# Four cross-attention layers in one kernel: layer 1 on a thread of its own, layer 2's weights folded, and new durations in the kernel's planner

## The chip, the cores and the metric

The kernel runs on one core of one Trainium2 chip. The metric is the device time of one execution, in microseconds (us). The core has a matrix engine (TensorE, "PE" in the profile; its weight loads are shown as "PEld"), a vector engine (VectorE, "DVE"), a scalar engine (ScalarE, "ACT"), a general engine (GpSimd, "POOL") and a queue that issues the transfers (SyncE, "SP"). Matrix products end in PSUM, a memory of eight banks; everything else lies in SBUF.

## The reference

`x` has 64 batches of 128 tokens by 128 features; the context `ctx` has 64 batches of 77 tokens by 128. Four layers follow each other, all in f32. Cut to what is computed:

```
# layer 0, 16 heads of 8
Q = x @ Wq.T + bq;  K = ctx @ Wk.T + bk;  V = ctx @ Wv.T + bv
s = where(causal, Q_h @ K_h.T / sqrt(8), -1e9)
x = layer_norm(softmax(s) @ V_h + x);  x = gelu(x @ W1.T + b1) @ W2.T + b2 + x
# layer 1, 16 heads of 8
s = where(mask, -inf, (q_h @ k_h.T / sqrt(8)) * attention_weights)   # both 64 x 16 x 128 x 77
x = layer_norm(x + (softmax(s) @ v_h) @ Wo.T + bo)
# layer 2, 16 heads of 8, one 8 x 8 matrix wq, wk, wv shared by all heads
s = where(mask == 0, -1e20, (x_h @ wq) @ (ctx_h @ wk).T)
a = layer_norm((softmax(s / sqrt(128)) @ (ctx_h @ wv)) @ w_out + b_out + x)
x = layer_norm(relu(a @ w_ff1 + b1) @ w_ff2 + b2 + a)
# layer 3, 16 heads of 64 over x itself, in segments of 64 tokens
q, k, v = split(rms_norm(x) @ to_qkv);  q, k = rope(q), rope(k)
x = x + softmax(mask(q @ [mem, persist, k].T / 8)) @ [mem, persist, v] @ to_out
x = x + (silu(g) * a) @ ff_w2 + b2,  a, g = split(rms_norm(x) @ ff_w1 + b1)
```

## The kernel before

The 64 batches are worked on in 16 groups of four. Within a group a layer's projections and its feed-forward run on all four batches at once (512 columns), its attention batch by batch.

**The planner.** The program is not written in the order in which it runs. Layers are Python generators. Each engine call is recorded by `Plan`, which gives it a time: `Plan.matmul` for PE (line 150), `Plan.other` for the other engines (line 237), from durations written down in those functions. `issue` (line 295) then emits every engine's instructions by planned time, and each engine runs its own list in that order. A generator yields what it needs next: `"wait"` and a condition, `"also"` and a new generator (a new thread), or a tile shape of PE with the tiles that must be ready. The loop at the end (line 1378) takes the thread whose need is met first. There are two chains of threads: chain 0 is layers 0 to 2, chain 1 is layer 3. The variable `ahead` (line 1380) weighs them, so that chain 0 stays `LEADS` groups of work in front, with `WORK` as one group's work. Where the planner expects PE to stand for over `FILL` = 0.4 us, `keep_busy` (line 198) puts in filler products that nothing reads (`mm<-first,ident` in the profile, 512 or 128 columns), in the tile shape of the product that is waited for.

**Tile shapes of PE.** A product with 32 rows of weights uses a quarter of the array (shape 32x128); 64x64, 128x64 and 128x32 occur too. `Plan.switch` (line 217) charges a change of shape.

**Layers 0 to 2.** `layers_0_to_2` (line 1296) is one thread: for each group it runs `layer1(g)`, then `layer0_attention(g + 1)` (for groups past the first three; groups 1 and 2 have a thread and tiles of their own, `early_layer0`), then `layer2(g)`. Outputs and feed-forwards are threads that it starts. All three use one set of tiles, `own` (line 443), and `attend` (line 663) lets the values of one attention begin only when those of the attention before it are through (`tiles.ready`).

**Attention.** `attend` makes, per batch, a masked copy of the keys (`keys_of`, POOL line 673), then twice (eight heads each) `scores`: two products of 32 rows each into two PSUM banks (line 705, f32, which PE runs in two passes), from one of two pairs of banks (tag `sc`). The penalty of masked keys is added by products first (line 696): in layer 2 with 32 rows of weights, in layer 0 with the full 128 rows (the identity times the causal penalty, both bf16), so the shape changes between the two lines. Then DVE takes the maximum (line 717) and subtracts it (line 718), and ACT takes the exponential of 616 columns (line 721). Layer 1 has `first` (line 1021) ahead of that, for each half: multiply by the weights (line 1022), overwrite masked places (line 1024). `values` turns the scores on PE (line 656), copies them with ACT (line 657), multiplies with the values (line 740), copies (line 749), turns back (line 755), and DVE normalises (lines 760 and 762).

**Layer 2's weights.** wq, wk and wv are laid out as block diagonals; keys, values and queries are projected (lines 612, 623, 642), and `w_out` is applied in `layer2_output`.

**Layer 3's values** (line 1131): the first 64 tokens are copied by ACT straight into `vext`, the other 64 into `vs` (line 1132) and from there into `vext` by a transfer (line 1133). Two transfers bring the memory's row (line 1136).

The planner's durations for DVE and ACT in the kernel before; `hidden` is the part of an instruction that the next on the same engine may overlap, also where it needs the first one's result:

```
        elif engine == "DVE":
            cost, hidden = 0.15 + n * (0.0066 if op == "reciprocal" else 0.00104), 0.075
...
        elif engine == "ACT":
            cost, hidden = 0.157 + n * 0.00083, 0.06
...
            own, end = t + takes, t + cost
```

Of the kernel before, what the change touches and what calls it, by code (L numbers as in the profile page):

```python
# [12 lines left out]
F32 = mybir.dt.float32  # L13
# [7 lines left out]
P = 128  # L21
# [32 lines left out]
WORK = 71.0  # L54
LEADS = (1.60, 1.60, 1.20, 1.60, 1.60, 1.60, 1.60, 1.60, 1.60, 1.30, 1.40, 1.60, 1.60, 1.60, 1.60, 1.60)


class Plan:
# [8 lines left out]
    SWITCH = {  # L67
        (128, 128): {(128, 64): 0.093, (64, 64): 0.092, None: 0.094},
        (32, 128): {None: 0.267},
        (128, 64): {(128, 128): 0.13, None: 0.15},  # L70
        (64, 64): {None: 0.13},
        (128, 32): {None: 0.174},
    }

    def __init__(self):
        self.records = []
        self.lines = {}
        self.past = {}
        self.free = {}
        self.tags = {}  # L80
        self.pe, self.shape, self.work = 0.7, (128, 128), 0.0
        self.window, self.use, self.clock = 0.0, 0.0, 1.0
        self.known = {}
        self.idle = None
        self.lost, self.switched, self.fills = 0.0, 0.0, 0
        self.block = 0.0, 0.0
# [63 lines left out]
    def matmul(self, dst, w, x, passes, call, line):  # L150
# [7 lines left out]
        if shape[0] == 32:  # L158
            cost *= 0.3125
        elif shape[0] == 64:  # L160
            cost = max(cost / 4, 0.028)
        elif shape[1] == 32:
            cost /= 4
        elif shape[1] == 64:
            cost = max(cost / 2, 0.028)
        else:
            cost = max(cost * 1.02, 0.05 if half else 0.109)
        cost *= passes
        self.work += cost
# [7 lines left out]
        self.run(start, shape, cost, call, line, self.waits("PE", ends))  # L177
        end = self.pe + (0.2 if self.clock == 1.0 else 0.3)
# [4 lines left out]
    def run(self, start, shape, cost, call, line, extra=0.0):  # L183
# [11 lines left out]
        self.pe = start + switch + cost  # L195
        self.shape = shape

    def keep_busy(self, until, shape, line):

# [17 lines left out]
    def switch(self, shape):  # L217
        if shape == self.shape:
            return 0.0
        costs = self.SWITCH[self.shape]  # L220
        return costs.get(shape, costs[None])
# [15 lines left out]
    def other(self, engine, op, args, kw, call, line):  # L237
# [7 lines left out]
        elif engine == "DVE":  # L245
            cost, hidden = 0.15 + n * (0.0066 if op == "reciprocal" else 0.00104), 0.075
            cost += {"stream_shuffle": 0.05, "scalar_tensor_tensor": 0.06}.get(op, 0.0)
            cost += 0.105 if op == "copy_predicated" else 0.0
        elif engine == "ACT":
            cost, hidden = 0.157 + n * 0.00083, 0.06  # L250
# [3 lines left out]
        else:  # L254
            cost, hidden = 0.05 + n * 0.0024, 0.02
            if op == "tensor_tensor" and n <= G:
                cost = 1.02
# [31 lines left out]
        else:  # L289
            own, end = t + takes, t + cost  # L290
# [54 lines left out]
def four_layers(ctx: ExitStack, tc: tile.TileContext, a: dict, out: bass.AP):  # L345
# [10 lines left out]
    def pool_of(name, dtypes={}, space=None, **tiles):  # L356
# [5 lines left out]
    store = pool_of("store", xs=(4, G * P))  # L362
# [5 lines left out]
        "att", {"fm": U8, "mi": I32}, kb=(2, CT), s=(3, H * S2), fm=(2, H * S2),  # L368
        s3=(2, H * KE), sT=(1, 12 * P), sT3=(1, H * P), w=(2, 2 * P), mi=(1, CT),
    )  # L370
    act = pool_of(
        "act", {"part": BF16}, xT=(2, G * P), x3=(2, G * P), o=(2, G * P), y=(1, G * P),
        y3=(2, G * P), part=(1, P),
# [69 lines left out]
    own = Tiles(  # L443
        xT=(act, "xT"), kT=(proj, "kT"), v=(proj, "v"), qT=(proj, "qT"), o=(act, "o"),
        kb=(att, "kb"), s=(att, "s"), sT=(att, "sT"), w=(att, "w"),
    )

# [161 lines left out]
    def keys_values(cT, wk, bk, wv, bv, name, tiles=own):  # L609
        yield F, cT, "mm"  # L610
        pk = bank([P, CT], f"{name}_pk")
        matmul(pk, wk, cT, start=True, stop=True)
        kT = tiles.tile("kT", [P, G, S2], f"{name}_k")
        if bk is None:
            acte.copy(kT.rearrange("p b k -> p (b k)"), pk)
        else:
# [5 lines left out]
        for b in range(G):  # L622
            matmul(pv[:, b, :], cT[:, b * S2 : (b + 1) * S2], wv, start=True, stop=True)
        v = tiles.tile("v", [S2, 4, G, QR], f"{name}_v")
        pv = pv.rearrange("p b (f w) -> p f b w", f=4)
        if bv is None:
            acte.copy(v, pv)
        else:
            bv = bv.rearrange("p (f w) -> p f w", f=4).unsqueeze(2)
# [33 lines left out]
    def attend(qT, kT, va, pen, load, first, scale, name, tiles=own):  # L663
# [7 lines left out]
        def keys_of(b):  # L671
            kbs[b] = tiles.tile("kb", [P, QD, S2], f"{name}_{b}_kb")
# [7 lines left out]
        def scores(b):  # L680
            n = f"{name}_{b}"
            kb, s = kbs[b], ss[b]
            if b + 1 < G:
                keys_of(b + 1)
            mx = small.tile([P, H], F32, tag="mx", name=f"{n}_mx")
            for half in range(2):
                h0 = 8 * half
                yield F if pen is not None and pen(b)[2] == P else (32, 128), kb, qT, s, "sc"
                pb = two_banks(f"{n}_ps{half}")
                ps = pb[:, :, : QD * S2].rearrange("p c (i k) -> p c i k", k=S2)  # L690
                if pen is not None:
                    for c in range(2):
                        r = slice(QR * (2 * half + c), QR * (2 * half + c) + pen(b)[2])
                        if pen(b)[2] == P:
                            r = slice(0, P)
                        matmul(
                            ps[:, c],
                            pen(b)[0][r],
                            pen(b)[1][r].unsqueeze(1).to_broadcast([r.stop - r.start, QD, S2]),
                            start=True,  # L700
                            stop=False,
                        )
# [11 lines left out]
                if first is not None:  # L714
                    first(b, h0, d, ps)
                    ps = d
                dve.tensor_reduce(m, ps, AX.X, ALU.max)  # L717
# [66 lines left out]
        keys_of(0)  # L784
# [17 lines left out]
    pen0 = load("c_causal0", [P, S2])  # L802
# [6 lines left out]
    pen016 = const.tile([P, S2], BF16, tag="pen016", name="pen016")  # L809
    dve.tensor_copy(pen016, pen0)  # L810

    def pen_causal(b):
        return ident16, pen016, P
# [37 lines left out]
    fed = [0]  # L851

    def layer0_feed_forward(g, o, ready):
# [8 lines left out]
        fed[0] = g + 1  # L862


    begun0 = layer0_attention(0, *inputs0)
# [17 lines left out]
    def block_diagonal(name):  # L883
        rep = load(name, [P, DH])
        t = const.tile([P, H, DH], F32, tag=f"d_{name}", name=f"d_{name}")
        pool.tensor_tensor(
            t,
            rep.unsqueeze(1).to_broadcast([P, H, DH]),
            hmask.unsqueeze(2).to_broadcast([P, H, DH]),
            ALU.mult,  # L890
        )
        return t.rearrange("p h d -> p (h d)")

    wq2, wk2, wv = (block_diagonal(f"L2_{x}") for x in ("wq", "wk", "wv"))
    wv2 = const.tile([P, 4, 4, DH], F32, tag="wv2", name="wv2")
    for f, (h, step) in enumerate(FOURS):
        pool.tensor_copy(
            wv2[:, f], wv.rearrange("p (h d) -> p h d", d=DH)[:, h : h + 3 * step + 1 : step]
        )
    wv2 = wv2.rearrange("p f g d -> p (f g d)")  # L900
    wo2 = load("L2_w_out", [P, 1, P], a["L2_w_out"].unsqueeze(1))
# [13 lines left out]
    pen3 = load("c_causal3", [P, KE])  # L915
    pen316 = const.tile([P, KE], BF16, tag="pen316", name="pen316")
    dve.tensor_copy(pen316, pen3)
    wmem = load("L3_to_mem_tokens_w", [P, P])
# [15 lines left out]
    def memory_tokens():  # L934
# [16 lines left out]
        vmem = const.tile([B, H, DH3 + 1], F32, tag="vmem", name="vmem")  # L951
# [4 lines left out]
        mn = const.tile([B, P], F32, tag="mn", name="mem_n")  # L956
        acte.activation(mn, pm, AF.Copy, scale=1.0 / S2)
        sq = const.tile([B, P], F32, tag="sq", name="mem_sq")
# [8 lines left out]
        pooled = const.tile([P, B], F32, tag="mn2", name="mem_pooled")  # L967
# [4 lines left out]
        tokT = const.tile([P, B], F32, tag="mn3", name="mem_tokT")  # L972
# [7 lines left out]
        dve.memset(vmem[:, :, DH3], float(NM))  # L980
        for c in range(2):
            yield F, tokT, "mm"
# [499 lines left out]
```

## Time and profile before

| | us |
|---|---|
| median of 3 runs (2543.57 to 2558.1) | 2552.77 |
| span of the profiled execution, first to last instruction | 2548.2 |
| PE busy in it | 2406.2 |
| DVE busy | 1893.3 |
| ACT busy | 1412.2 |
| POOL busy | 1286.6 |

The profile gives for each group of instructions its source line, engine, operation, the tiles written and read, its shape and count, then the summed busy time and the mean duration of one in ns, then the idle time of the engine ahead of them and what ended it. PE's products are pipelined, so their durations overlap: what one costs is read from the distance between starts, not from its duration. Only idle time of the engine that sets the end costs anything.

PE's instruction list of the program before has 16,470 products, of which 489 are fillers (372 of 512 columns, 117 of 128), and 1155 changes of tile shape. SP issues 745 transfers.

### The profile page before, as it was taken

What the parts mean: (1) busy time and instruction counts of PE and PEld (TensorE: products, weight loads), DVE (VectorE), ACT (ScalarE), POOL (GpSimd) and SP (SyncE); (2) the same over time, 40 slices, a digit from 0 to 9 for tenths busy, and PEclk for the clock granted to TensorE, in tenths of its full rate; (3) what the DMA queues carried; (4) which work ended last, traced back from release to release, by engine and by line L of the source; (5) the groups of instructions that cost most, each with busy time, mean ns of one, the idle gap of its engine ahead of it and who ended that gap; (6) DMA issues with size and microseconds to landing.
All of it is one profiled execution on the core that took longest, in us unless ns stands there. A gap on an engine that the chain in (4) does not pass through costs nothing.

```text
span 2548.2 us, 64630 instructions
## 1 busy us (share of the span) xinstructions
PE 2406.2 (94%) x26657; PEld 1786.3 (70%) x26657; DVE 1893.3 (74%) x3952; ACT 1412.2 (55%) x2489; POOL 1286.6 (50%) x1290
## 2 busy tenths in 40 slices
PE   7999999999999999999999999999999999999998
PEld 4565776768677677677676776777767667767776
DVE  3756886967868678786877768687787868867765
ACT  3454556565565645556565655656556565554553
POOL 2234554645555546453564546455455554536653
PEclk9999999999999999999999999999999999999999
DMA  5412212111121121212112121211112112120000
GB/s 111 122 33 44 65 20 46 46 34 39 43 43 42 35 48 25 67 21 56 35 27 62 25 65 21 51 39 40 41 32 51 34 35 55 21 60 13 14 22 15
DMA packets 376768, 108.23 MB, mean 42 GB/s; under 512 B 329027, under 2 KB 365208, under 8 KB 376344
## 3 DMA queue, kind: packets, MB, share of 16 engines
q1 hardware_dynamic: 376472, 104.08, 18.2%
q8 instruction: 210, 3.44, 0.6%
q14 instruction: 86, 0.70, 0.1%
HBM read 74.97 MB, written 4.19 MB: 31 GB/s over the span
## 4 chain that ended last, share of the span: by engine, by line
PE 53%; DVE 28%; issue 6%; POOL 5%; ACT 4%; DMA 2%; SPq 1%; DVEq 0%; POOLq 0%; ACTq 0%
PE mm L656 8%; PE sc L705 5%; PE mm L1099 5%; DVE mx L717 5%; PE mm L590 4%; PE sc L1195 3%; PE sc L845 3%; DVE s L718 3%; PE mm L740 3%; DVE s L1024 3%; PE mm L1226 2%; DVE s L1022 2%; DVE ro L1101 2%; PE mm L1129 2%; DVE mx L1167 2%
## 5 line engine op out<-in xcount | busy, mean ns | idle before, releaser
L657 ACT COPY sT<-mm 116x512 f32<-116x512 f32 (+2 forms) x832 | 442.8, 585 | 147.5 <-PE mm L656 138.6
L1102 POOL TENSOR_TENSOR ro<-ro,w_c_sin 128x512 f32<-128x512 f32 x256 | 328.0, 1281 | 354.2 <-DVE ro L1101 353.3
L656 PE MATMUL mm<-w_c_ident,s 128*116 128x128 f32 (+2 forms) x3328 | 458.2, 282 | 51.0 <-ACT sT L657 14.3
L721 ACT ACTIVATE s<-s 128x616 f32<-128x616 f32 x384 | 275.1, 717 | 399.0 <-DVE s L718 397.8
L656 PEld LDWEIGHTS mm<-w_c_ident,s 128*116 128x116 f32 (+2 forms) x3328 | 379.2, 146 | 133.5 <-issue 40.5
L673 POOL TENSOR_TENSOR kb<-kT,qmask 128x308 f32<-128x308 f32 x184 | 131.8, 726 | 413.6 <-PE sc L705 259.8
L717 DVE TENSOR_REDUCE mx<-sc 128x8 f32<-128x616 f32 x256 | 202.8, 792 | 111.0 <-PE sc L705 105.1
L541 POOL TENSOR_TENSOR rstd<-rstd,mhalf 128x4 f32<-128x4 f32 x96 | 99.3, 1035 | 364.3 <-DVE rstd L540 345.6
L1099 PE MATMUL mm<-x,w_L_to_qkv_w 128*128 128x128 f32 x2048 | 265.9, 280 | 5.4 <-ACT xT L533 1.5
L1099 PEld LDWEIGHTS mm<-x,w_L_to_qkv_w 128*128 128x128 f32 x2048 | 244.8, 193 | 29.0 <-issue 13.6
L705 PE MATMUL sc<-kb,qT 32*128 32x308 f32 x1472 | 248.3, 460 | 6.5 <-DVE s L1168 2.6
L718 DVE TENSOR_TENSOR s<-sc,mx 128x616 f32<-128x616 f32 x256 | 204.6, 799 | 9.1
L1101 DVE STREAM_SHUFFLE ro<-mm 128x512 f32<-128x512 f32 x256 | 188.3, 735 | 0.7 <-issue 0.3
L740 PE MATMUL mm<-sT,vf 116*32 116x128 f32 (+1 forms) x4608 | 175.8, 280 | 3.6 <-DMA vf<-o 1.1
L740 PEld LDWEIGHTS mm<-sT,vf 116*32 116x32 f32 (+1 forms) x4608 | 116.3, 110 | 76.8 <-issue 30.0
L1107 POOL TENSOR_TENSOR q<-q,ro 128x512 f32<-128x512 f32 x128 | 164.9, 1288 | 10.0
L1107 POOL TENSOR_TENSOR kext<-kext,ro 128x512 f32<-128x512 f32 x128 | 154.0, 1203 | 10.0
L1195 PEld LDWEIGHTS sc<-vext,sT 81*64 81x64 f32 x4096 | 128.9, 138 | 39.0 <-issue 17.4
L1022 DVE TENSOR_TENSOR s<-sc,s 128x616 f32<-128x616 f32 x128 | 101.5, 793 | 67.2 <-PE sc L705 63.2
L1195 PE MATMUL sc<-vext,sT 81*64 81x65 f32 x4096 | 142.6, 225 | 6.5 <-DVE s L1168 3.3
L705 PEld LDWEIGHTS sc<-kb,qT 32*128 32x128 f32 x1472 | 103.6, 188 | 58.6 <-issue 38.3
L1167 DVE TENSOR_REDUCE mx<-sc 128x8 f32<-128x648 f32 x128 | 105.7, 826 | 49.5 <-PE sc L1159 49.4
(224 smaller groups left out, 4690.8 us busy)
## 6 DMA issues: line engine op xcount, KB each, us to landing
s<-in_fside SPq DMA_DIRECT2D x64, 616.0 KB
vext<-vs SPq DMA_DIRECT2D x64, 256.0 KB
fm<-in_fmask SPq DMA_DIRECT2D x64, 154.0 KB
vf<-v SPq DMA_DIRECT2D x138, 38.5 KB
cT<-in_ctxT SPq DMA_DIRECT2D x32, 154.0 KB
xT<-in_xT SPq DMA_DIRECT2D x16, 256.0 KB
xs<-in_x SPq DMA_DIRECT2D x16, 256.0 KB
out<-y SPq DMA_DIRECT2D x16, 256.0 KB
```

Of the source, the lines that this page charges most:

```text
L656: transpose(pt[:, i, :], s[:, columns(keys, j + i)])
L657: acte.copy(dst[:keys, j : j + 4, :], pt)
L705: matmul(ps[:, c], qT[r, b * P : (b + 1) * P], kb[r], start=pen is None, stop=True,)
L717: dve.tensor_reduce(m, ps, AX.X, ALU.max)
L718: dve.tensor_tensor(d, ps, m.unsqueeze(3).to_broadcast([P, 2, QD, S2]), ALU.subtract)
L721: acte.activation(s[:, h0 : h0 + 8], s[:, h0 : h0 + 8], AF.Exp, scale=scale)
L740: matmul(pa[VC * c : VC * c + VC, x // 2, :], va[:r, x, b, c], sT[:r, j, :], start=x != 1, stop=x != 0,)
L1099: matmul(pq[:, j, :], w, xT, start=True, stop=True)
L1101: dve.stream_shuffle(ro, pq, swap)
L1102: pool.tensor_tensor(ro, ro, sinT.unsqueeze(1).to_broadcast([P, 4, P]), ALU.mult)
L1107: pool.tensor_tensor(d, d, ro, ALU.add)
L1195: matmul(pa[SEG * s : SEG * s + SEG, c, j, :], sT[:, slot, SEG * s : SEG * s + SEG], vx[:, s, head(slot), :], start=True, stop=True,)
```

## The change

1. **Threads.** `layers_0_to_2` becomes `layers_0_and_2`, which runs layer 0 of group g + 2 and layer 2 of group g, with a second set of tiles `others` from the same pools; `layer1s` is a thread of its own with the set `own`. Layer 1 drops its context after the keys and values, and layer 2 loads the context again.
2. **Pools.** One more `xs`, `kb`, `w`, `o` and `y`; one `y3` fewer; `mi`, the penalties' f32 copies and the memory tokens' scratch go into pool tiles.
3. **Layer 0's penalty** is made from 32-row products: three pieces of 32 keys for each of the two banks (128, 128 and 52 columns), in the shape of the scores that follow.
4. **Layer 1's softmax.** After both halves are multiplied, both are masked, both maxima taken, the maxima negated and scaled in one small DVE instruction, and ACT takes 16 exponentials of 77 columns with the maximum as bias. Line 718's subtraction goes away for layer 1.
5. **Layer 2's weights folded.** wq and wk become one 128x128 matrix, wv and w_out another, at the start of the kernel. Keys are not projected (the context is used as it is), and the context is turned instead of multiplied for the values, with two ACT copies for one.
6. **Layer 3.** All 128 tokens' values are copied into `vs` and both halves go by transfer into `vext`; the memory's row comes in four transfers for two.
7. **The planner.** Row groups of 32-row products get their own clocks (`rows`), so that products of different row groups are planned at the same time and other shapes wait for them; a change of shape costs `DRAIN + LOAD * columns`; other durations are revised; `WORK` and `LEADS` change.

```diff
-WORK = 71.0
-LEADS = (1.60, 1.60, 1.20, 1.60, 1.60, 1.60, 1.60, 1.60, 1.60, 1.30, 1.40, 1.60, 1.60, 1.60, 1.60, 1.60)
+WORK = (59.0, 60.5)
+LEADS = (2.4,) * 16
...
+        row = self.reach(w)[0] // QR if shape[0] == 32 else None
+        self.settle(row is None)
+        if row is not None:
+            cost = max(cost, 0.028)
...
+        if row is not None:
+            self.pe = max(start + switch, self.rows.get(row, 0.0))
+            self.rows[row] = self.pe + cost
+            self.pe += 0.007 * 2
...
-        costs = self.SWITCH[self.shape]
-        return costs.get(shape, costs[None])
+        return self.DRAIN + self.LOAD * shape[1]
...
-            cost, hidden = 0.15 + n * (0.0066 if op == "reciprocal" else 0.00104), 0.075
+            cost, hidden = 0.15 + n * (0.0066 if op == "reciprocal" else 0.00104), 0.083
+            late = 0.035
...
-            cost, hidden = 0.157 + n * 0.00083, 0.06
+            cost, hidden = 0.157 + n * 0.00083, 0.1
...
-            own, end = t + takes, t + cost
+            own, end = t + max(takes, cost + late if late else 0.0), t + cost
...
-        if bk is None:
-            acte.copy(kT.rearrange("p b k -> p (b k)"), pk)
+        kT = cT.rearrange("p (b k) -> p b k", k=S2)
+        if wk is not None:
...
-            matmul(pv[:, b, :], cT[:, b * S2 : (b + 1) * S2], wv, start=True, stop=True)
+            if wv is None:
+                transpose(pv[:, b, :], c)
...
+                    for j, c in [(j, c) for j in range(pen.count) for c in range(2)]:
+                        r = slice(QR * (2 * half + c), QR * (2 * half + c) + QR)
+                        w, x, k = pen(b, r, j)
+                        x = x.unsqueeze(1).to_broadcast([QR, QD, k.stop - k.start])
+                        matmul(ps[:, c, :, k], w, x, start=j == 0, stop=False)
...
+                    for h, _, _ in later:
+                        masked(b, h)
+                    for _, x, y in later:
+                        dve.tensor_reduce(y, x, AX.X, ALU.max)
+                    dve.tensor_scalar(mx, mx, -scale, None, ALU.mult)
+                    for h in range(H):
+                        acte.activation(s[:, h], s[:, h], AF.Exp, scale=scale, bias=mx[:, h : h + 1])
...
-            acte.copy(vx[0:SEG, 0, 8 * half : 8 * half + 8, 0:DH3], pv3[0:SEG])
-            acte.copy(vs[SEG:P, 8 * half : 8 * half + 8, :], pv3[SEG:P])
-        sp.dma_start(vx[0:SEG, 1, :, 0:DH3], vs[SEG:P])
+            acte.copy(vs[:, 8 * half : 8 * half + 8, :], pv3)
+        for s in range(2):
+            sp.dma_start(vx[0:SEG, s, :, 0:DH3], vs[SEG * s : SEG * s + SEG])
...
+    def layer1s():
+        for g in range(NG):
+            yield "wait", lambda: g in fed and plan.free["cT"] and (g - 2 in ended or g < 2)
+            begun[0] += 1
+            o, ready = yield from layer1(g, load_ctx(g), own)
+            yield "also", layer1_output(g, o, ready)
+
+    def layers_0_and_2():
...
+        yield "also", layer1s()
         for g in range(NG):
...
+                o, ready = yield from layer0_attention(g + 2, cT0, None, others)
+                yield "also", layer0_feed_forward(g + 2, o, ready)
             yield "wait", lambda: g in ys
+            ended.add(g)
+            o, ready = yield from layer2(g, ys.pop(g))
             yield "also", layer2_output(g, o, ready)
```

In the program's PE list, products other than fillers: 256 products of 128 rows (layer 0's penalty) are gone, 768 of 32 rows are new, 16 of layer 2's key projection are gone and 64 of its values have become turns. Fillers are now 761 (626 of 512 columns, 135 of 128), changes of tile shape 904. SP issues 953 transfers.

## The prediction

> **What bounds the kernel now.** I read the page's busy row and chain first, then PE's timeline, then the groups of DVE and ACT.
>
> ```profile
> span 2548.2 us, 64630 instructions
> PE 2406.2 (94%) x26657; PEld 1786.3 (70%) x26657; DVE 1893.3 (74%) x3952; ACT 1412.2 (55%) x2489; POOL 1286.6 (50%) x1290
> ...
> PE 53%; DVE 28%; issue 6%; POOL 5%; ACT 4%; DMA 2%; SPq 1%; DVEq 0%; POOLq 0%; ACTq 0%
> ```
>
> PE holds over half of the chain, DVE a quarter. But 94% is no measure of PE's real work, because products overlap. So I cut PE's timeline into blocks (products of one line and shape in a row), took a block's cost as the distance from its first start to the next block's first start, and called the 15th percentile of alike blocks (same line, number of products, with or without a change of shape behind) its unhindered cost. PE's 2540 us from first to last product are then 2164 us of unhindered blocks, 119 us of fillers (489, with what they wait) and 257 us of stalls: waits of some 0.05 to 2.5 us all over the span.
>
> The blocks that the change touches most are the scores. Timeline of PE (start, length, line, shape, count in passes):
>
> ```profile
> 1000.43 0.33 PE L696 MATMUL sc<-pen,first 32*128 32x308 bf16 x4
> 1000.57 0.70 PE L705 MATMUL sc<-kb,qT 32*128 32x308 f32 x8
> 1001.21 0.86 PE L740 MATMUL mm<-sT,vf 116*32 116x128 f32 x24
> ...
> 1007.08 0.31 PE L696 MATMUL sc<-pen,first 32*128 32x308 bf16 x2
> 1007.23 0.68 PE L705 MATMUL sc<-kb,qT 32*128 32x308 f32 x4
> 1007.83 0.66 PE L755 MATMUL mm<-w_c_ident,w 128*128 128x128 f32 x4
> ```
>
> Two halves of layer 2's scores back to back take 1001.21 - 1000.43 = 0.78 us; one alone takes 1007.83 - 1007.08 = 0.75. Four row groups run at once, so the second half is nearly free. In layer 0 it never is:
>
> ```profile
> 1105.74 0.43 PE L696 MATMUL sc<-pen,ident 128*128 128x308 bf16 x2
> 1106.10 0.79 PE L705 MATMUL sc<-kb,qT 32*128 32x308 f32 x4
> 1106.82 2.94 PE L1099 MATMUL mm<-x,w_L_to_qkv_w 128*128 128x128 f32 x24
> ```
>
> The penalty in full shape takes 0.36 us and the scores 0.72 behind it, half by half.
>
> DVE's timeline in layer 1:
>
> ```profile
> 1062.60 0.79 DVE L1022 TENSOR_TENSOR s<-sc,s 128x616 f32<-128x616 f32 x1
> 1063.42 0.91 DVE L1024 COPY_PREDICATED_SCALAR s<-fm,far 128x616 f32 x1
> 1064.37 0.79 DVE L717 TENSOR_REDUCE mx<-s 128x8 f32<-128x616 f32 x1
> ```
>
> Each depends on the one before and starts 0.03 us after its end (0.82 and 0.95 apart). The planner of before lets the next start 0.075 us ahead of the end (`hidden`), so it plans DVE 0.109 us too fast for each such pair. The trace has some 1060 of these pairs: 116 us of DVE time that the planned order doesn't know of. Line 718 in layer 1 adds 128 x (0.935 - 0.791 planned) = 18. Together 134.
>
> ```profile
> L718 DVE TENSOR_TENSOR s<-s,mx 128x616 f32<-128x616 f32 x128 | 119.6, 935 | 4.4
> ...
> L721 ACT ACTIVATE s<-s 128x616 f32<-128x616 f32 x384 | 275.1, 717 | 399.0 <-DVE s L718 397.8 <-DVE vmem L980 0.2
> ...
> L576 ACT ACTIVATE y<-xs,rstd 128x128 f32<-128x128 f32 x128 | 41.2, 390 | 42.3 <-POOL rstd L541 42.3
> ```
>
> **The change, part by part.**
> *Score blocks.* Unhindered costs by median: one half without penalty 0.718, with layer 2's 0.756; two halves 0.730 and 0.778. Before, PE's list has 193 single halves without penalty of its shape (layer 0's among them), 68 with, 32 doubles without and 30 with: 138.6 + 51.4 + 23.4 + 23.3 = 236.7, and 128 full-shape penalties x 0.359 = 46.0, in all 282.7. After, the list has 46, 26, 37 and 52 of these (33.0 + 19.7 + 27.0 + 40.5) and for layer 0 37 singles and 48 doubles (48 x 0.778 + 37 x 0.756 = 65.3) plus x for each of these 85 blocks, as three weight loads and three short products stand in each row group for one. x is not in the trace. Below: two more products of 128 columns, without waiting for weights, would take some 0.07 (the 308-column one hides its successor's load: 0.15 from its start to the scores). Above: each added load fully seen at its median of 90 ns, and the scores' own load as well, 0.25. I take 0.15, between: 12.8. Sum 198.3, so -84 (-91 to -76).
>
> [...]
>
> *Changes of shape.* Leaving the full shape costs 0.094 us (four turns 0.437, with a change behind 0.530). Full-shape exits fall from 470 to 345: -11.8. Exits from 128x64 fall by 21 at 0.148, from 64x64 by 3 at 0.10: -3.4.
>
> *Layer 2's fold.* Line 612 x 16 groups x 0.521 = -8.3. Values: eight passes (0.873) become four turns (0.437): -7.0. Folding itself adds eight products at the start, some 1.5.
>
> *Fillers* are counted from the list: 254 more of 512 columns at 0.216 and 18 of 128 at 0.056: +56. They mark idle time that the new planner expects; they cost PE only what would be idle anyway, but that idle time is in the span.
>
> So PE's work falls by 84 + 11.8 + 3.4 + 15.3 - 1.5 = 113, and known idle time grows by 56.
>
> *Stalls, 257 now.* The new durations charge dependent DVE pairs their end plus 0.035, and line 718 leaves layer 1, so the 134 us of unplanned DVE time are planned or gone. DVE holds 28% of the chain; 28% of 134 is 38, all of it 134. I take 50, nearer the low end because PE ends more of the chain. No gain from it, or a loss, can't be excluded: see the rivals.
>
> *Other engines,* off the path, hidden behind PE's 2400 us. DVE: 128 x 0.935 less, 64 small ones x 0.18 more: -108, 1785. ACT: 128 exponentials of 616 columns less (-92), 1024 of 77 more. Nearest row is line 576 (128 columns, an operand per partition: 390 ns, four of them 1.26 us, so 0.29 apart); 51 columns fewer at most 0.04 less, so 0.25 to 0.29 each, +256 to +297. The values' copies of lines 1131 and 1132 are halved (-74), layer 2's -6.5 + 4. ACT 1412 to between 1500 and 1540, 62% of the new span. POOL's counts are the same. SP issues 208 transfers more (64 of 256 KB, 128 small, 16 contexts): queue 1 is busy 18.2% of 16 engines for 104 MB, 17 MB more are 3%. PE's waits for a transfer after the start are 1 us in the table of waits (line 740), and `vext` has two buffers, filled a batch ahead: 0. If that cover failed, a late SP would hold line 1195, once per batch.
>
> [...]
>
> Sum: 2548.2 - 113 + 56 - 50 = 2441. The profiled execution's own time isn't among the three shown; its span lies 4.6 under their median, which I add for what surrounds it: **2445**.
>
> **The rivals.**
> *A. The late DVE was behind most stalls.* All 134 go: 2445 - 84 = 2361. For: ACT's biggest wait (398 us) is for line 718, and DVE's share of the chain. Against: fillers rise, so the new planner sees idle time that it can't remove.
> *B. The saved PE work comes back as idle time.* Chains wait on each other through the three score tiles and two `vf`, now shared by two attentions at once; stalls grow by 57 instead of falling by 50: 2445 + 107 = 2552. For: the fillers' +56 show half of the saving going that way already. Against: a separate layer 1 gives the loop more threads to choose from.
> *C. Slower: bursts on ACT.* Sixteen exponentials in a row hold ACT 16 x 0.25 = 4.0 us; the longest single one now is line 1174's 1.28. Behind them stand the copies of turned scores (line 657) that free PE's four banks. From 107/64 = 1.7 us of stall a batch the gain is gone; at 2.6 the time is 2445 + 64 x 2.6 = 2611. Against: ACT idles 45%, and the planner charges each of the 16 its own time (0.36, with 0.1 hidden), so it orders around bursts.
> *D. The penalty's pieces don't overlap* (the edit doesn't do what it says): 12 loads at 90 ns one after the other for a double, six for a single: x is 1.08 and 0.54, 72 us instead of 13: 2445 + 59 = 2504. Against: the loads of 32-row products now start 3 to 10 ns apart.
>
> **How the numbers follow.** Forecast 0.50 (its own range 2395 to 2500: x, stalls down by 0 to 100), A 0.20, D 0.09, B 0.09, C 0.12. A measurement of this kernel tells about 0.5%, 13 us, from no change. Faster: 0.50 + 0.20 + 0.09 and a third of B, 0.82; same 0.05; slower 0.13. The range takes in most of A and D, and leaves out B from its middle on and C: 2350 to 2530.
>
> **What would show it.** Line 712's and 715's blocks together some 200 us, doubles of layer 0 at 0.9 us; fillers near 175; stalls by the same cut near 207; line 736's exponentials 0.25 to 0.29 apart; PE's waits for ACT copies no longer than now. I am wrong if stalls don't fall, or if line 671's copies wait behind line 736.

## The result, and the profile after

| | median, us | range of the runs | ratio to before, 95% interval |
|---|---|---|---|
| before | 2552.35 | 2543.57 to 2558.1 | |
| after | 2574.66 | 2568.49 to 2580.1 | 1.0096 [1.0068, 1.0123] |

The change makes the kernel 22 us slower, where 107 us less was forecast. The page of the kernel after, with its busy row, the granted TensorE clock in 40 slices, and the shares of the chain that ended last:

```profile
span 2578.3 us, 67248 instructions
...
PE 2419.2 (94%) x27355; PEld 1827.2 (71%) x27355; DVE 1783.1 (69%) x3899; ACT 1493.3 (58%) x3256; POOL 1265.5 (49%) x1286
...
PEclk8899799999899997999999999999999999999999
...
PE 61%; DVE 19%; ACT 10%; POOL 4%; issue 4%; DMA 1%; SPq 1%; DVEq 0%; POOLq 0%; ACTq 0%
PE mm L670 9%; ACT s L736 6%; PE mm L599 6%; PE mm L1156 5%; PE sc L715 5%; PE mm L761 4%; PE sc L880 3%; PE sc L1254 3%; PE mm L1285 3%; PE mm L1186 2%; DVE mx L738 2%; DVE s L739 2%; PE sc L1218 2%; PE mm L1279 2%; DVE s L1075 2%
```

DVE's busy time is where the forecast put it (1783 for 1785), ACT's just below (1493 for 1500 to 1540), and DVE's share of the chain fell from 28% to 19%. PE and ACT took over: PE holds 61% for 53%, ACT 10% for 4%, of which the new exponentials (line 736) are 6%. The clock row has changed too: before, all 40 slices stand at 9, now five lie below. Mean granted clock: 0.986 before, 0.952 after.

The same cut of PE's timeline as in the prediction, with the stalls divided by whether the clock was halved beside them (us, first to last product; "lead" is the time before the first product):

| | span | lead | unhindered | fillers | stalls at half clock | other stalls | time at half clock |
|---|---|---|---|---|---|---|---|
| before | 2548.2 | 3.8 | 2164 | 119 | 42 | 215 | 72 |
| forecast for after | 2441 | 3.8 | 2051 | 175 | 207 together | | |
| after | 2578.3 | 14.3 | 2051 | 176 | 122 | 211 | 246 |

The two counted terms came out as forecast: unhindered work -113, fillers +57. (That the first agrees to the microsecond is luck: blocks grouped a little differently give -92 to -104.) The error is in stalls, 333 where 207 were forecast, and in 10 us more ahead of the first product. Stalls grew by 76 us: those that touch stretches at half clock by 80, while the others fell by 4.

PE's timeline of after, start, length, line, shape and count. First two halves of layer 0's scores with the penalty in 32 rows:

```profile
1320.47 0.37 PE L712 MATMUL sc<-ident,pen 32*128 32x128 bf16 x10
1320.63 0.50 PE L715 MATMUL sc<-kb,qT 32*128 32x308 f32 x2
1320.68 0.19 PE L712 MATMUL sc<-ident,pen 32*128 32x52 bf16 x2
1320.71 0.76 PE L715 MATMUL sc<-kb,qT 32*128 32x308 f32 x6
1321.40 0.66 PE L776 MATMUL mm<-w_c_ident,w 128*128 128x128 f32 x4
```

1321.40 - 1320.47 = 0.93 for both halves together; the full-shape penalty and scores took 1.08 for one. That part did what it says. Further on, the same kind of block with fillers in it, and then PE's busy time, that of PEld, DVE, ACT and POOL, and the granted clock by stretches:

```profile
693.69 0.45 PE L712 MATMUL sc<-ident,pen 32*128 32x128 bf16 x6
693.96 1.38 PE L715 MATMUL sc<-kb,qT 32*128 32x308 f32 x4
695.13 7.46 PE L712 MATMUL mm<-first,ident 32*128 32x512 bf16 x17
701.96 0.45 PE L712 MATMUL sc<-ident,pen 32*128 32x128 bf16 x6
```

```profile
698.00:708.00 10.00, 10.00 (x69) 5.98 (x68) 2.69 (x5) 2.26 (x6) 0.70 (x1) 0.54 0.01 2
708.00:718.00 10.00, 10.00 (x143) 7.58 (x142) 4.17 (x8) 5.95 (x11) 0.00 (x0) 1.00 0.01 2
```

Two things to see. `keep_busy` plans a 512-column filler of under 128 rows at half the price of a full one, 0.107 us, so 17 of them were planned as 1.8 us at the full clock. At the 0.216 that this trace shows from one start to the next at the full clock (147 pairs of 32 rows) they would be 3.7; they hold PE for 6.83 (695.13 to 701.96), as the clock stands at half from 686.8 to 707.2, where the same distance is 0.427, and the next scores stand behind them. And PE is busy through all of 698 to 708 and yet runs at 0.54 of the clock: with these fillers it did not come back, and only at 707.2, 5 us after their end, did it. The start, with the idle time ahead in brackets:

```profile
14.27 0.48 PE L839 MATMUL mm<-w_c_ident,y 128*128 128x128 f32 x1 [14.27 <-DVE y L838]
...
19.39 9.40 PE L938 MATMUL mm<-first,ident 128*128 128x512 bf16 x45
37.73 0.84 PE L938 MATMUL mm<-w_c_ident,y 128*128 128x128 f32 x2 [8.95 <-POOL y L930]
...
41.76 0.37 PE L712 MATMUL sc<-ident,pen 32*128 32x128 bf16 x10
```

PE took its list in order here. The penalty's turns (line 839) stand first in it, after 14.27 us of idle time, and the folding (line 938), ahead of which PE sits idle for 8.95 us until POOL's block diagonals are there, stands ahead of layer 0's first scores. Those scores begin at 41.8 us; before, the first penalty product was at 15.1.

### The profile page after: what moved, and what is told of

It is laid out like the page before. It is cut to its first block, busy times and chain, and to the rows that moved or that the text cites. A ratio compares the mean times of both kernels' runs of the same rounds, so it can differ in the third digit from the quotient of the medians.

```text
span 2578.3 us, 67248 instructions
## 1 busy us (share of the span) xinstructions
PE 2419.2 (94%) x27355; PEld 1827.2 (71%) x27355; DVE 1783.1 (69%) x3899; ACT 1493.3 (58%) x3256; POOL 1265.5 (49%) x1286
## 4 chain that ended last, share of the span: by engine, by line
PE 61%; DVE 19%; ACT 10%; POOL 4%; issue 4%; DMA 1%; SPq 1%; DVEq 0%; POOLq 0%; ACTq 0%
PE mm L670 9%; ACT s L736 6%; PE mm L599 6%; PE mm L1156 5%; PE sc L715 5%; PE mm L761 4%; PE sc L880 3%; PE sc L1254 3%; PE mm L1285 3%; PE mm L1186 2%; DVE mx L738 2%; DVE s L739 2%; PE sc L1218 2%; PE mm L1279 2%; DVE s L1075 2%
## 5 line engine op out<-in xcount | busy, mean ns | idle before, releaser
L670 PE MATMUL mm<-w_c_ident,s 128*116 128x128 f32 (+2 forms) x3328 | 474.3, 288 | 34.4 <-ACT s L736 6.3
L670 PEld LDWEIGHTS mm<-w_c_ident,s 128*116 128x116 f32 (+2 forms) x3328 | 393.4, 149 | 127.8 <-issue 49.3
L736 ACT ACTIVATE s<-s,mx 128x77 f32<-128x77 f32 x1024 | 262.8, 348 | 59.6 <-DVE mx L734 59.0
L742 ACT ACTIVATE s<-s 128x616 f32<-128x616 f32 x256 | 182.2, 716 | 178.3 <-DVE s L739 176.5
L715 PE MATMUL sc<-kb,qT 32*128 32x308 f32 x1472 | 221.0, 480 | 9.6 <-DVE s L739 4.4
L688 POOL TENSOR_TENSOR kb<-kT,qmask 128x308 f32<-128x308 f32 x120 | 83.6, 708 | 270.3 <-PE sc L715 141.9
L770 ACT COPY w<-mm 128x256 f32<-128x256 f32 x184 | 68.1, 370 | 140.6 <-PE mm L761 136.4
```

The costliest lines, as they stand in the source:

```text
L670: transpose(pt[:, i, :], s[:, columns(keys, j + i)])
L715: matmul(ps[:, c], qT[r, b * P : (b + 1) * P], kb[r], start=pen is None, stop=True,)
L736: acte.activation(s[:, h], s[:, h], AF.Exp, scale=scale, bias=mx[:, h : h + 1])
```

## The experiments

The order of work comes out of a planner, so any edit reorders everything behind it. Each run is therefore judged by its time and by the cut, and two runs (c_l20, e_line_fill22) change nothing but the order, to show how much the order alone does. What the change did to other durations of the planner (the clocks of row groups, the price of a change of shape) and layer 3's new transfers were not varied alone. In runs where a line is added, line numbers shift by one or more.

**a_full: all fillers in full shape** (the changed kernel otherwise).

```diff
     def keep_busy(self, until, shape, line):
...
+        shape = (P, P)
         product, w, x = self.idle
```

> The changed kernel with one line more: fillers always have the full shape of 128x128, whatever product they wait for (506 fillers, 87 us by 0.216 and 0.056 us each, where the changed kernel has 761 and 143 us, 336 of them in 32x128). Theory T1 (the fillers' shape: products of 32 rows don't hold PE's clock, and a filler of 512 columns in 32 rows takes 0.216 us where the planner counts 0.107): half-clock time falls from 248 us to 100 or less, stalls that touch half-clock time from 122 to some 50, the time from 2575 to 2440 to 2490. Theory T2 (bursts of 16 exponentials on ACT stall PE): the time moves by the fillers at most, 2520 to 2575, and half-clock time stays over 180 us. Theory T3 (only the late start costs): 2560 to 2580.

**a_cost: the fillers keep their shapes, but their true length is planned.**

```diff
-            cost = n * 0.00041667 * (1.0 if rows == P else 0.5)
+            cost = n * 0.00041667
```

> The changed kernel, but the planner counts a filler of fewer than 128 rows with its true 0.216 us for 512 columns and so puts in half as many (548 fillers, 96 us; those of 32x128 fall from 64 to 31 us). The shape of the fillers stays. T1 has two halves, and this takes away one: if it is overlong filling that costs, the time falls by 40 us or more and half-clock time stays near 250 us; if it is the clock, half-clock time stays at 200 us or more and the time falls by less than 50 us, to 2530 to 2575. T2 and T3: 2550 to 2580.

**b_quarter: the kernel before with every filler in 32 rows**, and **b_full: the same with every filler in full shape** (the line of a_full, in b_quarter with `(QR, P)`).

> The kernel before the change with every filler in the shape 32x128 (836 fillers, 164 us by 0.216 and 0.056 each, where it has 489 and 87 us, 91 of them in 32x128); nothing else is changed. T1: half-clock time rises from 74 us to over 200, and the time from 2552 by 60 us or more, to 2610 to 2720. If the shape of a filler doesn't matter for the clock, half-clock time stays under 100 us and the time rises by no more than the overlong filling, 20 to 80 us.

> The kernel before with fillers of the full shape (418 fillers, 74 us; 91 of its 489 had 32x128). T1 in small: half-clock time from 72 us to 50 to 75 and the time from 2552 by 5 to 25, to 2527 to 2547. Otherwise 2545 to 2560.

| | median, us | ratio, 95% interval | fillers, us | stalls at half clock / other | at half clock |
|---|---|---|---|---|---|
| a_full | 2515.99 | 0.9854 [0.9837, 0.987] | 134 | 93 / 205 | 150 |
| a_cost | 2544.14 | 0.9965 [0.9946, 0.9984] | 142 | 114 / 214 | 224 |
| b_quarter | 2700.28 | 1.0585 [1.0563, 1.0607] | 224 | 82 / 218 | 264 |
| b_full | 2539.91 | 0.996 [0.9946, 0.9974] | 117 | 40 / 217 | 72 |

One line takes 59 us off the changed kernel and makes it faster than before, though less than expected (2440 to 2490, and at most 100 us at half clock, where it has 150). It changes the fillers' price with their shape, and besides those of 32 rows also 138 of 64x64 and 63 of 128x64. About half of the gain (30 us) comes with the true price alone; the rest needs the shape, for a_cost still spends 224 us at half clock. The same line brings 12 us in the kernel before, which has few fillers of 32 rows (no more than a new order alone moves, see c_l20); giving it nothing but those costs 148 us. Some half of these 148, too, are price: the 836 fillers take 164 us at the full clock, those of before 87. The rest goes with 192 us more at half clock. b_quarter's longest row of fillers, and PE's windows in it (columns as above):

```profile
308.53 36.61 PE L1160 MATMUL mm<-first,ident 32*128 32x512 bf16 x92
```

```profile
310.00:320.00 10.00, 10.00 (x28) 3.59 (x27) 0.73 (x2) 0.00 (x0) 9.67 (x10) 0.57 0.27 16
320.00:330.00 10.00, 10.00 (x24) 3.38 (x23) 0.00 (x0) 0.00 (x0) 0.00 (x0) 0.50 0.00 0
330.00:340.00 10.00, 10.00 (x25) 3.53 (x24) 0.00 (x0) 0.00 (x0) 0.00 (x0) 0.50 0.00 0
```

PE is never idle here, and the clock goes to half and stays there past the end of the fillers at 345.1 (0.55 over 340 to 350). So this row of 32-row fillers didn't keep the clock. The same shows over whole traces. In before and after, each stretch at half clock (17 and 41 of them) lasts a whole multiple of 3.41 us (1 to 8 of them), and so does each at the full clock in between. I took the windows of that length in which products cover 80% or more, by the share of the window that 32-row products cover, from before, after and b_quarter together (a product counted with the time that its columns take, 0.216 us for 512 of bf16, and not with its longer duration in the profile; how exactly it is counted moves these numbers a little, but not their order):

```
32-row share of the window   at full clock: windows, of these the next one at half
below 0.5                    1404, 0
0.5 to 0.8                     21, 6
0.8 and over                   20, 17
```

In after, 12 of the 41 losses of the clock follow a window that products cover by over 0.55 (the highest 0.97); in a_full none of 32 does (the highest 0.53). The other losses follow windows that products cover by about half or less.

**a_late: the folding on a thread behind layer 0's first attention, the penalty's turns behind its first projections.** The fillers stay as the change has them.

```diff
+        begun0_at = next(begun0)
+    for j in range(3):
+        pt = bank([P, P], f"pen0_p{j}")
...
-    wqk2 = folded("wqk2", ("L2_wq", True), ("L2_wk", True))
-    wvo2 = folded("wvo2", ("L2_wv", True), (None, False)).unsqueeze(1)
+    def all_folds():
+        yield from folded("wqk2", ("L2_wq", True), ("L2_wk", True))
+        yield from folded("wvo2", ("L2_wv", True), (None, False))
...
+        yield "also", all_folds()
         yield "also", layer1s()
...
-            yield "wait", lambda: g in ys
+            yield "wait", lambda: g in ys and len(folds) == 2
```

> The changed kernel, where layer 2's weights are folded by a thread that starts behind the first attention of layer 0, and the penalty's turns stand behind the first projections in PE's list; fillers as in the changed kernel. The first product of scores starts at 41.8 us in the changed kernel and at 16.3 before. T3 (the start): it falls to 16 to 20 us and the time from 2575 by 20 to 28, to 2547 to 2555, if nothing else moves; PE's fillers fall from 143 to 108 us of planned time besides, so 2520 to 2555. If the start is made up for later, 2565 to 2580.

**a_fix: a_full and a_late together.**

> Full-shape fillers and the late folding and turns together. T1 and T3 both, adding up: 2516 less some 25, so 2475 to 2500; half-clock time under 150 us. If the two are the same loss twice, 2505 to 2520.

a_late: 2489.59, 0.9765 [0.9729, 0.9801]; a_fix: 2484.68, 0.9746 [0.9714, 0.9777]. The start of a_fix:

```profile
13.14 2.04 PE L657 MATMUL mm<-xT,w_L_WqT 128*128 128x512 f32 x2 [4.05 <-DMA w_L_WqT<-in_L_WqT]
14.98 0.42 PE L900 MATMUL mm<-w_c_ident,y 128*128 128x128 f32 x1
...
17.70 0.68 PE L713 MATMUL sc<-ident,pen 32*128 32x128 bf16 x6
```

The first scores come at 17.7 for 41.8, 24 us earlier; a_fix is 31 us below a_full. a_late gained more than its expectation allowed, 85 us, and the two edits don't add up: taken the other way round, the start is worth 85 and the full shape behind it only 5. With its start, a_late's plan also changed its fillers, from 176 us to 148, and its time at half clock from 246 to 183, so part of a_full's gain seems to have come by another order. The two together, 90 us, are measured. How they divide is not: the timeline's 24 us and the 31 of a_fix against a_full are the best figures for the start.

**a_oldsm and c_oldsm: layer 1's softmax as before the change**, first in the changed kernel, then in a_fix.

```diff
-                    later.append((h0, d, m))
-                    if half == 0:
-                        continue
...
-                    for h in range(H):
-                        acte.activation(s[:, h], s[:, h], AF.Exp, scale=scale, bias=mx[:, h : h + 1])
-                    break
+                    masked(b, h0)
```

> The changed kernel with layer 1's softmax as before the change (mask, maximum, subtraction per half on DVE, two exponentials of 616 columns on ACT), all else as changed. T2 (the bursts cost): 2500 to 2550, and PE's waits for ACT copies fall. T1: DVE has 100 us more work and dependent steps again and the planner puts in more fillers (982, 183 us, 93 of them in 32x128), so 2580 to 2640.

> This is a_fix with layer 1's softmax as before the change (the row's maximum subtracted by DVE, two wide exponentials). Theory 1 (PE sets the end, and ACT's bursts of 16 exponentials cost about what DVE's saved subtraction brings): within 15 us of a_fix, 2470 to 2500 us. Theory 2 (the bursts hold up the copies that PE waits for): 2440 to 2465 us. Theory 3 (the subtraction was in the way of layer 1's chain): 2505 to 2540 us; the list's 575 fillers, 17 us more than a_fix's, speak for this one.

a_oldsm: 2578.97, 1.0105 [1.0089, 1.012], the changed kernel's own time. c_oldsm: 2516.32, 0.9868 [0.9852, 0.9883], 32 us above a_fix: its list has 1084 changes of shape for 967, unhindered work is 2086 for 2057 and fillers 164 for 131, stalls 256 for 288. So ACT's bursts aren't what made the change slow, and with the fillers right the new softmax gains. In the changed kernel that gain didn't show. The bursts may not be free, though: by the cut the stalls in the blocks that turn the scores (line 670, which waits for line 736) are some 100 us in the changed kernel and some 65 in a_oldsm. There the planner's fillers, 232 us for 176, take the difference back.

**c_dve0 and b_dve: DVE's durations in the planner.** c_dve0 is a_fix with the old ones, b_dve is b_full with the new ones.

```diff
-            cost, hidden = 0.15 + n * (0.0066 if op == "reciprocal" else 0.00104), 0.083
-            late = 0.035
+            cost, hidden = 0.15 + n * (0.0066 if op == "reciprocal" else 0.00104), 0.075
```

> This is a_fix with DVE's prices as the planner of before had them (the next instruction may start 0.075 us ahead of the end even when it depends on it; nothing added behind the end). My prediction said that planning the true DVE times takes 50 us of stalls away. Theory 1 (that step holds, only hidden by the clock in the first result): without the prices a_fix loses it again, 2520 to 2550 us, and stalls on PE rise by some 50. Theory 2 (planning late DVE work makes PE's waits known but doesn't shorten them: what was a stall becomes a filler or a wait for another engine): 2470 to 2500 us, within 15 us of a_fix's 2484.7; the program has 402 fillers where a_fix has 445, 7.5 us less of known idle time, and stalls are higher by about that much.

> This is b_full (the kernel before with full-shape fillers, 2539.9 us) with the changed kernel's DVE prices, and nothing else. Theory 1 (true DVE prices take 50 us of stalls away): 2480 to 2505 us. Theory 2 (they only make the waits known): the list has 639 fillers where b_full has 418, 38 us more of known idle time; stalls fall by about as much, and the time stays at 2525 to 2555 us.

c_dve0: 2525.9, 0.9901 [0.9886, 0.9915], 41 us above a_fix: stalls 335 for 288, fillers 124 for 131. b_dve: 2553.42, 1.0009 [0.9999, 1.0019], 13.5 us above b_full: stalls 218 for 257, but fillers 152 for 117 and unhindered work 2173 for 2162. In both kernels the true durations take 39 to 47 us of stalls away. In the new one some 40 of the 47 touch half clock (164 us at half clock in c_dve0, 120 in a_fix), so it is not shown that shorter waits for DVE were the cause. In the old one known idle time and more unhindered work (the list has 1253 changes of shape for 1169) take all of it back; in the new one they don't.

**c_l20: a_fix with a lead of 2.0 groups for 2.4.**

> This is a_fix with the lead of layers 0 to 2 over layer 3 planned at 2.0 groups where it had 2.4: the same work in another order, to see how much the order alone moves the time. The list has 608 fillers (103 us) where a_fix has 445 (77 us). If known idle time counts in full and the rest stays: 2510 us. If the order alone scatters the waits by tens of us whichever way: anywhere from 2460 to 2540, with other stalls away from a_fix's 231 us by over 20.

2497.88, 0.979 [0.9769, 0.9812]: 13 us above a_fix, with 39 us more of fillers and 26 us less of stalls.

**d_line: a_fix with layer 1 back in the loop's line**, so that one attention of layers 0 to 2 follows the other (groups 0 to 2 of layer 0 aside). **e_line_only** is the same edit in the changed kernel as it is.

```diff
-        yield "also", layer1s()
         for g in range(NG):
+            yield "wait", lambda: g in fed and plan.free["cT"]
+            begun[0] += 1
+            o, ready = yield from layer1(g, load_ctx(g), own)
+            yield "also", layer1_output(g, o, ready)
             if early < g + 2 < NG:
```

> This is a_fix with layer 1 put back in the loop's own line: layer 1 of a group, then layer 0 two groups on, then layer 2, one attention at a time instead of two (pools, folding and durations stay). a_fix's products are 105 us shorter than before's, but its stalls are 31 us longer than before's. Theory 1 (two attentions at once wait on each other, for the score tiles, the two vf and for ACT and DVE): stalls fall below before's 257 and the time is 2440 to 2470 us. Theory 2 (the thread gives the planner more to choose from and so keeps stalls down): 2510 to 2570 us, with stalls over 310. Theory 3 (the thread makes no difference; fewer us of products to lie beside make the other engines' chains show): 2470 to 2500 us.

> The changed kernel with layer 1 back in the loop's line, and its fillers and its start as the change left them. Theory 1 (the thread costs 25 us by itself, as between a_fix and d_line): 2540 to 2560 us. Theory 2 (the gain of d_line is one lucky order; the thread as such costs nothing): 2565 to 2600 us. The list has 68.6 us of fillers in 32 rows (the changed kernel 64), so the clock lost should be about as much, half-clock time 200 to 290 us.

d_line: 2459.46, 0.9637 [0.9618, 0.9656]. e_line_only: 2521.2, 0.9897 [0.9872, 0.9921]. The thread of its own costs 25 us in a_fix and 53 in the changed kernel (the medians; the profiled execution of e_line_only was its fastest):

| | span | unhindered | fillers | stalls at half clock / other | at half clock |
|---|---|---|---|---|---|
| a_fix | 2483.5 | 2057 | 131 | 57 / 231 | 120 |
| d_line | 2457.1 | 2059 | 132 | 63 / 194 | 113 |
| after | 2578.3 | 2051 | 176 | 122 / 211 | 246 |
| e_line_only | 2510.9 | 2049 | 178 | 66 / 199 | 145 |

Work and fillers are equal in each pair; only stalls differ. e_line_only was expected at 2540 or more; its fillers of 32 rows are as many as after's, but it loses the clock far less, which I can't explain from the counts. The head of the table of PE's waits (tile, line, releaser; us, times, longest), a_fix first, then d_line:

```profile
PE sc L713 <- DVE s L740: 15.0, 20, 5.4
PE mm L942 <- POOL y L933: 13.7, 1, 13.7
PE mm L671 <- ACT sT L672: 9.0, 12, 2.4
PE mm L777 <- ACT w L771: 6.6, 15, 1.1
PE sc L1261 <- DVE s L740: 4.7, 6, 2.6
PE sc L716 <- DVE s L740: 4.6, 9, 1.0
```

```profile
PE sc L713 <- DVE s L740: 13.1, 17, 4.2
PE mm L942 <- POOL y L933: 13.0, 1, 13.0
PE mm L762 <- ACT sT L672: 8.9, 11, 3.6
PE mm L671 <- ACT sT L672: 7.4, 13, 2.1
PE mm L1193 <- ACT sT L672: 6.8, 6, 1.9
```

Waits for DVE's subtraction (line 740, which frees the score banks) lead in a_fix, and summed over all of PE's lines they fall from 25.5 us to 17.2 in d_line; those for ACT's copies of turned scores (line 672) rise from 21.0 to 28.5. By the cut, the stalls in the blocks that turn the scores (line 671) fall from 86 to some 70. This fits in part two attentions that hold each other up at the score tiles. But all of PE's waits in the profile fall by 14 us only (158 to 144), and no run varied the score tiles alone: why the thread costs what it does stays open.

**d_y3o: two y3 and two o for one and three; d_fill: fillers in gaps from 0.25 us for 0.4; e_line_fill: d_line and d_fill together; e_line_fill22: that with a lead of 2.2.**

```diff
-        "act", {"part": BF16}, xT=(2, G * P), x3=(2, G * P), o=(3, G * P), y=(2, G * P),
-        y3=(1, G * P), part=(1, P),
+        "act", {"part": BF16}, xT=(2, G * P), x3=(2, G * P), o=(2, G * P), y=(2, G * P),
+        y3=(2, G * P), part=(1, P),
...
-    FILL = 0.4
+    FILL = 0.25
```

> This is a_fix with two y3 tiles and two o tiles where it has one and three. The change took y3 from two to one; y3 holds a group's layer 3 on its way through the feed-forward. Theory 1 (the single y3 makes PE wait): 2440 to 2470 us and fewer stalls than 288. Theory 2 (layer 3 has other threads to run meanwhile, and a third o is worth more): 2490 to 2530 us; the list's 586 fillers, 23 us more than a_fix's, speak for it.

> This is a_fix with fillers in every planned gap of over 0.25 us where it was 0.4. a_fix still has 120 us at half clock, and 57 us of its stalls touch them. Theory 1 (short gaps in a row lower the weighted share of activity enough to lose the clock): half-clock time falls below 80 us and the time is 2455 to 2475 us. Theory 2 (the clock is lost in waits that the planner doesn't know of, and 51 more fillers don't lie there): 2475 to 2495 us, half-clock time 100 to 140 us.

> d_line and d_fill together: layer 1 in line, full-shape fillers in gaps from 0.25 us, the folding and the penalty's turns behind the start. If both gains stand beside each other: 2459.5 - 6.7 = 2453 us, with half-clock time below 100 us. If the shorter gaps don't matter: 2459 us.

> e_line_fill with a lead of 2.2 groups: another order of the same work, to see how far the order alone moves this version. From c_l20 against a_fix (13 us for 0.4 groups): within 15 us of e_line_fill, 2440 to 2470 us.

d_y3o: 2547.0, 0.9978 [0.9966, 0.999], 62 us above a_fix. The single y3 isn't what costs; whether the third o is worth so much or the order fell badly isn't told apart. d_fill: 2477.97, 0.9713 [0.9688, 0.9739], 7 us below a_fix with 99 us at half clock for 120. e_line_fill: 2462.77, 0.9659 [0.9642, 0.9676], and e_line_fill22: 2470.09, 0.9691 [0.967, 0.9713]: the shorter gaps bring d_line nothing. The two runs that changed only the order moved 7 and 13 us, so d_fill's 7 can't be told from it. A new order can do more, as a_late (85 us for a start worth 24 to 31) and perhaps d_y3o show. So the 59 and 31 us rest on what they do to the fillers, the clock and the start besides the time, and the thread's 25 on both pairs going the same way.

d_line is the fastest of all: 93 us below before, 115 below the changed kernel.

## Why the prediction was wrong

- *Score blocks, -84.* Right. Doubles of layer 0 take 0.930 in the median, x = 0.152 (0.15 taken); singles 0.848, x = 0.09. Rival D is out.
- *Changes of shape, fold, -30 together; fillers, +56.* Right in sum: unhindered -113, fillers +57. But the step said that fillers "cost PE only what would be idle anyway", and that failed. I priced the new fillers of 32 rows at 0.216 each and never asked what the planner had charged for them: 0.107. So the list holds up to twice the filler that a gap takes, and the products behind wait for it. a_cost puts that at 30 us: 34 us of fillers go, and the stalls stay (328 for 333).
- *Stalls, 257 to 207.* Here it failed, in three places. (1) The clock: nothing in the prediction prices it, though fillers exist to keep it. 336 of the new list's 761 fillers have 32 rows (91 of 489 before), and in these traces 17 of the 20 windows made up of 32-row products lost it; stalls at half clock went from 42 to 122. a_full takes 59 us away, the price above among them (5 us only, once the start is mended). (2) The thread: I noted under rival B that two attentions would share the score tiles, and took the fact that there are more threads to choose from as speaking against it. It costs 25 to 53 us, all in stalls; how, stays open. (3) DVE's true durations, the step's own reason, are worth 47 us of stalls against my 50 (c_dve0), but only measured against the changed kernel without them, and mostly in stalls at half clock. The level of 257 that I subtracted from belonged to another order. c_dve0 stands at 335.
- *The start.* "Folding itself adds eight products at the start, some 1.5": the products, yes. What stands behind them in PE's list while they wait for POOL, and the penalty's turns for DVE, was left out. 24 us by the timeline, 31 by a_fix against a_full, 85 by a_late with what its new order brought.
- *Other engines.* Right in their busy time, but "off the path" holds no longer for ACT, with 10% of the chain for 4%. The 16 exponentials:

```profile
L736 ACT ACTIVATE s<-s,mx 128x77 f32<-128x77 f32 x1024 | 262.8, 348 | 59.6 <-DVE mx L734 59.0 <-DMA vext<-vs 0.3
```

348 ns each, 0.250 apart, the low end of my 0.25 to 0.29. The turns' waits for line 671's copies fell from 14.3 us to 5.0, so rival C is out by the sign that I set for it; a_oldsm, as slow without the bursts, says the same. What I hadn't asked is whether the turns wait for the exponentials themselves. On the chain they do (line 736 holds 6%, where line 721 held 1%), though the idle time of PE that they end ahead of the turns is no longer than before, 6.3 us for 7.4.
- *Rival B* (saved work comes back as idle, 2552) comes nearest to what happened. Its place, two attentions at once, was right, but its 57 us of stalls were not enough without the clock and the start.

With the fillers, the start and the thread undone (59, 31 and 25 us in this order, other shares in another) the kernel takes 2459.46, 0.6% above the forecast. That closeness is part luck: d_line has 257 us of stalls, not the 207 forecast, and 132 us of fillers, not 175. The sum of the work was right, and the forecast took for granted that the program would be free to use it.

## What to carry to other kernels

A product that is there only to keep the matrix engine's clock is best given the full tile shape, and planned at its true length (here 0.216 us, where 0.107 was planned): fillers in full shape and at that price took 59 us off the changed kernel, and both errors hide, because the engine shows as busy. Setup that is moved into an in-order list is priced by what stands behind it while it waits (here 24 us by the timeline, for eight products of some 1.5 and the penalty's turns), not by its own length. And stalls of one order can't be carried over to another by adding and subtracting: take the new list, and ask for each new wait and filler what its planner believed.

## What the hardware showed that I had not expected

A busy PE did not always hold its clock. With products covering 80% or more of a 3.41 us window, 17 of 20 windows made up of 32-row products lost the clock and none of 1404 with less than half of them; b_quarter's clock stood at 0.50 for 20 us with PE busy in every one of them. In after, counting the time of 32-row products as a quarter orders the windows that lose the clock below those that keep it in 99.3% of pairs, counting it in full in 87%. The quarter is a fit: weights up to a half order them about as well, and no run varied the fillers' rows between 32 and 128. The clock also fell after windows that were far from idle: in a_full after ones that products cover by up to 0.53.

A filler of 512 bf16 columns took PE 0.216 us at the full clock and 0.427 at half, from one start to the next, whether it had 32 rows (147 and 48 pairs in after) or 128 (158 and 5). So fillers of 32 rows, all in the same row group, saved no time here, and cost the clock as well.
